# A graph network's first layer, written as a straight pass over chunks with more buffers between the engines

## The chip, the cores and the metric

The kernel runs on one core of a Trainium2 chip. A core has five engines with instruction queues of their own: PE (TensorE, the matrix unit), DVE (VectorE), ACT (ScalarE), POOL (GpSimd) and SP (SyncE). Each works its queue in order, and they meet only through semaphores. DMAs are issued from the queues of SP, ACT and POOL; a gather by a list of row numbers is issued on POOL. SBUF is the on-chip memory of 128 partitions, PSUM the memory that PE writes. The metric is the time of one execution on the device in microseconds (us).

## The reference

The program is four layers of message passing over a graph with 12,500 nodes and 400,000 edges, sorted by target `dst`; a node has 32 features. Ahead of each layer the features are normalized and passed through a relu. Only the first layer matters here:

```python
h = jnp.maximum(_layernorm(x, axis=-1), 0.0)
x = x + _L0_gnn_ref(h, edge_attr_32, L0_gnn_eps, src, dst)

def _L0_gnn_ref(node_feat, edge_feat, eps, src, dst):
    m = jax.nn.relu(node_feat[src] + edge_feat)
    neigh = jax.ops.segment_sum(m, dst, num_segments=node_feat.shape[0])
    return (1.0 + eps[0]) * node_feat + neigh
```

For each edge: fetch the source's row, add the edge's 32 numbers, relu, and add the result to the target's row. The third layer needs the number of edges of each source node (`deg`), which depends on `src` alone, so the kernel counts it in the first layer's pass.

## The kernel before

Edges lie 128 to a tile, one to a partition. There are 3125 tiles of real edges; 16 tiles (`CT`) make a chunk, four tiles (`G`) a group, four groups (`CG`) a chunk, and 196 chunks the pass. Since edges are sorted by target, and a chunk holds 2048 edges, the targets of a chunk lie within 128 consecutive rows, its window; the place of an edge in the window is prepared in `local`, with the window's first row as an integer in the last column (`wbase`). A flag read at the start chooses this fast way (`self.fast`) or a general one, which does not run with these inputs.

For each group the fast pass does this:

- Four indirect DMAs on POOL (L544 in `gather`) fetch 128 rows of 32 numbers each into the tile `hs`.
- `places0`: ACT makes the one-hot tile `oh` (128 edges x 128 places for each of four tiles): four squares of iota minus place (L472) and a relu of 1 - 2x over all of it (L473). What is 0 in the square becomes 1, all else 0.
- `main`: DVE adds `hs` and the edge's numbers into `m` (L678), ACT applies the relu (L679).
- `collect`: four matmuls of `m` with `oh` (L457), in float32, add up in the PSUM tile `ps_win` over the chunk; each shows as two records. The result stands transposed, 32 x 128.
- In `tail` (L684 on), the counting: DVE makes two one-hots in bfloat16, `ohi` and `olo` (L696), of the source's number split into quotient and remainder by 100 (`hi` and `lo`, made by `split_sources`, L480 to L483, once a chunk), and four matmuls (L699) add up their products in the PSUM tile `ps_deg`.

A chunk closes in its last group: ACT copies the sums to `s4` (L461), PE transposes them with an identity matrix (L462), ACT copies the 128 x 32 result to `wsum` (L464), and `put_late` has ACT read the window's first row into a register (L508) and issue the DMA that writes `wsum` into one of four tables of partial sums, which are added after the pass. DVE adds `ps_deg` to `deg` (L702).

The order is set by `edges`, a loop of a single round whose body is written out for all 784 groups. In step g it issues the gathers of group g+4 (`AHEAD`), the one-hots `oh` of group g+1, the message of group g, and the collecting and counting of group g-1. Loads by SP (`src`, `edge_attr_32` and `local`) run up to two chunks (`LEAD`) further ahead. In every second step after the first 16 one step of work for later layers (`rest`) is put in: loads, splits of float32 into bfloat16 parts, unit vectors. That order is the program's; a scheduler then places each engine's instructions by dependences and free buffers, and adds the semaphores.

The buffers between the engines are rotating: a tile's name has so many places, and a new tile waits until the instructions that read the one in its place are done. They are: `hs` six groups; `oh` and `m` three groups; `ohi` and `olo` two groups; `hi`, `lo` and `s4` two; `wsum` four; `ps_win` and `ps_deg` two chunks each; the loads six chunks.

Of the kernel before, what the change touches and what calls it, by code (L numbers as in the profile page):

```python
# [8 lines left out]
F32 = mybir.dt.float32  # L9
BF16 = mybir.dt.bfloat16  # L10
# [46 lines left out]
class GNN:  # L57
# [393 lines left out]
    def collect(self, l, pool, psum, c, feat, t0):  # L451

        nc = self.nc
        if t0 == 0:
            c["sum"] = psum.tile([P, P + D], F32, name="ps_win")
        for k in range(G):
            nc.tensor.matmul(c["sum"][:D, :P], lhsT=feat[:, k, :], rhs=c["oh"][:, k, :],  # L457
                             start=t0 + k == 0, stop=t0 + k == self.CT - 1)
        if t0 + G == self.CT:
            s4 = pool.tile([D, P], F32, name="s4")  # L460
            nc.scalar.copy(s4, c["sum"][:D, :P])  # L461
            nc.tensor.matmul(c["sum"][:, P:], lhsT=s4, rhs=self.eye[:D, :D], start=True, stop=True)  # L462
            s = pool.tile([P, D], F32, name="wsum", bufs=4)
            nc.scalar.copy(s, c["sum"][:, P:])  # L464
            self.put_late(l, c, s)

    def places0(self, pool, c, t0):

        nc = self.nc
        c["oh"] = pool.tile([P, G, P], F32, name="oh", bufs=3)  # L470
        for k in range(G):
            nc.scalar.activation(c["oh"][:, k, :], self.iota, AF.Square, bias=c["local"][:, t0 + k : t0 + k + 1], scale=-1.0)  # L472
        nc.scalar.activation(c["oh"], c["oh"], AF.Relu, bias=self.one, scale=-2.0)  # L473

    def split_sources(self, pool, c):

        nc, J, CT = self.nc, self.J, self.CT
        hi = c["hi"] = pool.tile([P, CT], F32, name="hi")
        lo = c["lo"] = pool.tile([P, CT], F32, name="lo")
        nc.vector.tensor_scalar(hi, c["src"], -0.5 * (J - 1), 1.0 / J, op0=ALU.add, op1=ALU.mult)  # L480
        nc.vector.tensor_scalar_add(hi, hi, ROUND)
        nc.vector.tensor_scalar_add(hi, hi, -ROUND)
        nc.vector.scalar_tensor_tensor(lo, hi, -float(J), c["src"], op0=ALU.mult, op1=ALU.add)  # L483

# [150 lines left out]
    def layer0(self):  # L635
        nc, tc, J = self.nc, self.tc, self.J
        if not self.fast:
            with tc.tile_pool(name="rest", bufs=1) as pool:
                for _ in self.rest(pool):
                    pass  # L640
        with ExitStack() as ctx:
            rest = None
            if self.fast:
                rest = self.rest(ctx.enter_context(tc.tile_pool(name="rest", bufs=1)))
                for _ in range(TABS[0]):
                    next(rest)
            big = ctx.enter_context(tc.tile_pool(name="big0", bufs=LEAD + 4 if self.fast else 2))
# [4 lines left out]
            flat = ctx.enter_context(tc.tile_pool(name="flat0", bufs=1, space=PSUM))  # L652
            iota = flat.tile([P, P], F32, name="iota_p")
            nc.vector.tensor_copy(iota, self.iota)

            def load(col):
                if self.fast:
                    c = {n: self.load(big, n, col) for n in ("src", "edge_attr_32")}
                else:
                    c = {n: self.load(big, n, col) for n in ("src", "dst", "edge_attr_32")}  # L660
                    c["row"] = self.load_row(big, "dst_t", col)
                    c["rows"] = big.tile([P, self.CT], I32, name="rows")
                c["col"] = col
                return c
# [890 lines left out]
```

## Time and profile before

| what | us |
|---|---|
| median of 3 runs | 20930.95 (20918.97 to 20951.87) |
| the profiled execution | 20928.96 |
| its span | 20927.2 |
| first gather of the first layer | 92.8 |
| last gather of the first layer | 4733.3 |
| last copy to `wsum` of the first layer | 4758.6 |
| first gather of the next stage | 4877 |
| POOL's gathers of the first layer, busy | 3029.8 |
| mean clock granted to TensorE over the span | 0.739 of full |

The span runs from the first to the last instruction on the core. The first layer takes the first 4.7 ms of 20.9; layers two and three together reach to about 15,300 us, and the last layer fills the rest. A row of the groups of instructions has the line in the kernel, the engine, the operation with output and inputs, the count, the busy time and the mean duration of one in ns, and then the idle time of the engine just before them, with what ended it. "Issue" is idle time in which the engine waited for nothing that the profile shows; "remote" is a release that the profile could not put down to an instruction. PEld is the loading of weights into PE, which overlaps its matmuls. POOL's row for a gather is the time to issue it, and its data arrive later.

### The profile page before, as it was taken

The page shows a single profiled execution, that of the slowest core. Times are in us where ns is not written, and L with a number is a line of the kernel's source. Part 1 is how long each engine was busy: PE and PEld are TensorE (multiplying, and loading weights), DVE is VectorE, ACT ScalarE, POOL GpSimd, SP SyncE. Part 2 cuts the span into 40 slices and gives each one's busy share as a digit, 9 for nine tenths or more (in the row PEclk, how much of TensorE's full clock was granted, in tenths as well). Part 3 has the DMA queues.
Part 4 walks back from the last instruction along what each step waited for, and adds up shares of the span by engine and source line. Part 5 has one row for each costly group of instructions (what it writes and reads, how often), then busy time and mean ns, then how long its engine had stood idle before and what let it go on. Part 6 is the DMA issues. An engine that isn't in the chain of part 4 may idle for free.

```text
span 20927.2 us, 193298 instructions
## 1 busy us (share of the span) xinstructions
PE 12665.5 (61%) x56836; PEld 6400.1 (31%) x56836; DVE 12158.2 (58%) x22370; ACT 7811.2 (37%) x17960; POOL 14371.0 (69%) x12508
## 2 busy tenths in 40 slices
PE   3344444434766666666666666666637777777776
PEld 2233333221211111111111111111135555555554
DVE  3333333224766666666666666666746666666666
ACT  2334444332333333333333333333224444444443
POOL 4666666664788888888888888888755555555553
PEclk6555555556777777777777777777768888888887
DMA  2113332112444444444444444444411111111111
GB/s 93 40 43 110 111 97 80 24 23 74 98 90 90 90 90 90 90 90 91 88 90 90 91 90 90 87 90 91 93 35 23 23 22 23 23 23 23 23 23 30
DMA packets 1538780, 1407.21 MB, mean 67 GB/s; under 512 B 1112166, under 2 KB 1307312, under 8 KB 1482824
## 3 DMA queue, kind: packets, MB, share of 16 engines
q1 hardware_dynamic: 724998, 1146.69, 17.4%
q0 software_dynamic: 750000, 205.60, 12.0%
q10 hardware_dynamic: 62704, 42.42, 0.7%
q8 instruction: 448, 7.34, 0.1%
q14 instruction: 630, 5.16, 0.1%
HBM read 1156.82 MB, written 236.20 MB: 67 GB/s over the span
## 4 chain that ended last, share of the span: by engine, by line
DVE 24%; PE 15%; issue 13%; another core or an unknown queue 13%; POOL 11%; ACT 7%; DMA 2%; DVEq 0%; ACTq 0%; SPq 0%; POOLq 0%
DVE z L862 6%; POOL acc L1017 5%; POOL hs L818 5%; PE ps_w L1316 5%; PE ps_y L859 4%; DVE pv L1324 1%; ACT oh L1346 1%; DVE f L1333 1%; DVE pa L1320 1%; PE ps_o L869 1%; ACT X L843 1%; ACT hid L1293 1%; DVE cnt L999 1%; PE ps_sum L1352 1%
## 5 line engine op out<-in xcount | busy, mean ns | idle before, releaser
L1017 POOL DMA_INDIRECT acc<-summed,rows x3125 | 5133.6, 1643 | 995.0 <-issue 886.7
L1280 POOL DMA_INDIRECT hs<-feat,src x3125 | 3008.8, 963 | 2498.0 <-DVE ps L1322 1494.4
L544 POOL DMA_INDIRECT hs<-feat,src x3125 | 3029.8, 970 | 1702.6 <-issue 863.1
L818 POOL DMA_INDIRECT hs<-feat,src x3125 | 3197.8, 1023 | 1195.8 <-issue 945.8
L1316 PE MATMUL ps_w<-w2b,hid 128*128 128x256 f32 x12544 | 3199.8, 412 | 70.5 <-issue 56.8
L862 DVE TENSOR_TENSOR z<-ps_y,hid 128x1024 f32<-128x1024 f32 x2352 | 2837.6, 1214 | 435.3 <-PE ps_y L859 164.6
L859 PE MATMUL ps_y<-X,w2t 64*128 64x512 f32 x4704 | 2377.1, 743 | 1129.8 <-DVE z L862 648.8
L1316 PEld LDWEIGHTS ps_w<-w2b,hid 128*128 128x128 f32 x12544 | 2578.0, 209 | 638.6 <-issue 89.8
L859 PE MATMUL ps_y<-Q,w2t 64*128 64x512 f32 x4704 | 1683.7, 840 | 1642.9 <-DVE z L862 1153.7
L491 ACT CAST f<-f 128x512 bf16<-128x512 f32 x784 | 479.9, 612 | 4773.9 <-DVE f L887 3739.1
L457 PE MATMUL ps_win<-oh,m 128*32 128x128 f32 x6272 | 1430.3, 406 | 819.5 <-ACT m L679 426.6
L869 PE MATMUL ps_o<-z,sums 128*32 128x512 f32 x9408 | 1748.1, 702 | 27.7 <-DVE r L874 16.1
L472 ACT ACTIVATE oh<-iota,local 128x128 f32<-128x128 f32 x3136 | 1018.6, 389 | 1923.2 <-remote 1520.1
L1293 ACT ACTIVATE hid<-ps_h 128x1024 f32<-128x1024 f32 x784 | 800.5, 1021 | 2390.6 <-remote 1992.0
L699 PE MATMUL ps_deg<-olo,ohi 128*125 128x100 bf16 x3136 | 432.6, 287 | 1793.5 <-DVE olo L696 1469.7
L1320 DVE TENSOR_TENSOR pa<-ps_w,q 128x512 f32<-128x512 f32 x784 | 539.9, 689 | 1650.4 <-remote 1476.6
L859 PEld LDWEIGHTS ps_y<-Q,w2t 64*128 64x128 f32 x4704 | 521.9, 256 | 2897.5 <-DVE z L862 1562.2
L833 DVE STREAM_TRANSPOSE X<-hs 128x512 f32<-128x512 f32 x392 | 273.4, 700 | 1943.4 <-DMA hs<-feat,src 1171.6
L859 PEld LDWEIGHTS ps_y<-X,w2t 64*128 64x128 f32 x4704 | 613.2, 210 | 2329.1 <-DVE z L862 1134.0
L457 PEld LDWEIGHTS ps_win<-oh,m 128*32 128x32 f32 x6272 | 946.1, 163 | 1157.6 <-ACT m L679 487.5
L678 DVE TENSOR_TENSOR m<-hs,edge_attr 128x128 f32<-128x128 f32 x784 | 226.9, 289 | 1642.8 <-remote 808.1
L1346 ACT ACTIVATE oh<-iota,local 128x128 bf16<-128x128 f32 x3136 | 1057.3, 391 | 50.7 <-DMA edge_attr<-in_edge_attr 26.3
(212 smaller groups left out, 19053.9 us busy)
## 6 DMA issues: line engine op xcount, KB each, us to landing
has<-loc_t SPq DMA_DIRECT2D x392, 1024.0 KB
srow<-in_src_t SPq DMA_DIRECT2D x392, 512.0 KB
hs<-feat,src POOLq DMA_INDIRECT x9375
N<-n_t SPq DMA_DIRECT2D x3136, 32.0 KB
emb<-pp SPq DMA_DIRECT2D x252, 280.0 KB
emb<-emb SPq DMA_DIRECT2D x196, 360.0 KB
emb<-pp SPq DMA_DIRECT2D x252, 224.0 KB
emb<-emb SPq DMA_DIRECT2D x196, 288.0 KB
```

What stands on the lines that cost most here:

```text
L457: nc.tensor.matmul(c["sum"][:D, :P], lhsT=feat[:, k, :], rhs=c["oh"][:, k, :], start=t0 + k == 0, stop=t0 + k == self.CT - 1)
L472: nc.scalar.activation(c["oh"][:, k, :], self.iota, AF.Square, bias=c["local"][:, t0 + k : t0 + k + 1], scale=-1.0)
L544: self.nc.gpsimd.indirect_dma_start(out=t[:, k, :], out_offset=None, in_=self.feats[l][:], in_offset=bass.IndirectOffsetOnAxis(ap=idx[:, t ...
L818: nc.gpsimd.indirect_dma_start(out=c["hs"][:, k, :], out_offset=None, in_=self.feats[1][:], in_offset=bass.IndirectOffsetOnAxis(ap=c["src" ...
L859: nc.tensor.matmul(y[:, q, :], lhsT=self.w2t[64 * q : 64 * q + 64, h, j, :], rhs=c["Q" if j < 3 else "X"][64 * q : 64 * q + 64, h, :], sta ...
L862: nc.vector.tensor_mul(z, y, c["hid"][:, 2 * h : 2 * h + 2, :])
L869: nc.tensor.matmul(c["o", j // 3][32 * q : 32 * q + 32, :], lhsT=self.sums[:, j, :], rhs=c["z", j, q % 2][:, q // 2, :], start=j % 3 == 0, ...
L1017: nc.gpsimd.indirect_dma_start(out=self.tabs[2][k % NTAB][:], out_offset=bass.IndirectOffsetOnAxis(ap=c["rows"][:, G * g + k : G * g + k + ...
L1280: nc.gpsimd.indirect_dma_start(out=c["hs"][:, k, :], out_offset=None, in_=self.feats[3][:], in_offset=bass.IndirectOffsetOnAxis(ap=c["src" ...
L1293: nc.scalar.activation(c["hid"][:, m, :, 2 * h : 2 * h + 2, :].rearrange("p b q s -> p q b s"), t.rearrange("p q (b s) -> p q b s", s=32), ...
L1316: nc.tensor.matmul(w[:, k, :], lhsT=c["hid"][:, m, 4 * g + k].rearrange("p q s -> p (q s)"), rhs=self.w2b[:, m, :], start=m == 0, stop=m == 1)
L1346: nc.scalar.activation(c["oh"][:, k, :], self.iota, AF.Square, bias=c["local"][:, k : k + 1], scale=-1.0)
```

## The change

The first layer's fast pass no longer goes through `edges`. A new function, `edges0`, writes it out by chunks, with pools of its own; the general way stays in `any0`. Each chunk has one `hs` tile of 16 x 32 numbers a partition, in four places, and its gathers are issued two chunks ahead, one group beside each group computed; loads go three chunks ahead. The tiles `oh`, `m`, `ohi` and `olo` have ten places each, `hi`, `lo` and `s4` three, `ps_win` and `ps_deg` three each. In a group the order is: gathers, one-hots `oh`, message, counting, collecting, all of the same group. The deg add, the copy to `s4` and the transpose of a chunk are issued after the third group of the next chunk, the copy to `wsum` and the write after its fourth. The instructions themselves and their shapes stay as they were.

```diff
-    def collect(self, l, pool, psum, c, feat, t0):
...
-    def places0(self, pool, c, t0):
...
-    def split_sources(self, pool, c):
...
     def layer0(self):
+        nc = self.nc
+        if self.fast:
+            self.edges0()
+        else:
+            self.any0()
+        with self.tc.tile_pool(name="end0", bufs=1) as pool:
+            agg = self.gather_sum(0, pool)
+            nc.vector.tensor_add(self.x, self.x, agg)
+            nc.vector.scalar_tensor_tensor(self.x, self.h, self.eps1, self.x, op0=ALU.mult, op1=ALU.add)
++    def edges0(self):
+
+        nc, tc, J, CT, NW = self.nc, self.tc, self.J, self.CT, self.NW
+        with ExitStack() as ctx:
+            rest = self.rest(ctx.enter_context(tc.tile_pool(name="rest", bufs=1)))
+            for _ in range(TABS[0]):
+                next(rest)
+            ld = ctx.enter_context(tc.tile_pool(name="load0", bufs=6))
+            gp = ctx.enter_context(tc.tile_pool(name="gather0", bufs=4))
+            mp = ctx.enter_context(tc.tile_pool(name="group0", bufs=10))
+            wp = ctx.enter_context(tc.tile_pool(name="work0", bufs=3))
+            psum = ctx.enter_context(tc.tile_pool(name="psum0", bufs=3, space=PSUM))
+            hist = ctx.enter_context(tc.tile_pool(name="hist0", bufs=3, space=PSUM))
+            flat = ctx.enter_context(tc.tile_pool(name="flat0", bufs=1, space=PSUM))
+            iota = flat.tile([P, P], F32, name="iota_p")
+            nc.vector.tensor_copy(iota, self.iota)
+
+            def fetch(c):
+                c["src"] = self.load(ld, "src", c["col"])
+                c["ea"] = self.load(ld, "edge_attr_32", c["col"])
+                c.update(self.places_of(ld, c["no"]))
+
+            def gather(c, g):
+                if g == 0:
+                    c["hs"] = gp.tile([P, CT, D], F32, name="hs")
+                    self.rows_for(c["hs"], CT, c, 0)
+                for k in range(G * g, min(G * g + G, self.filled(c))):
+                    nc.gpsimd.indirect_dma_start(
+                        out=c["hs"][:, k, :], out_offset=None, in_=self.feats[0][:],
+                        in_offset=bass.IndirectOffsetOnAxis(ap=c["src"][:, k : k + 1], axis=0))
+
+            def split(c):
+                hi = c["hi"] = wp.tile([P, CT], F32, name="hi")
+                lo = c["lo"] = wp.tile([P, CT], F32, name="lo")
+                nc.vector.tensor_scalar(hi, c["src"], -0.5 * (J - 1), 1.0 / J, op0=ALU.add, op1=ALU.mult)
+                nc.vector.tensor_scalar_add(hi, hi, ROUND)
+                nc.vector.tensor_scalar_add(hi, hi, -ROUND)
+                nc.vector.scalar_tensor_tensor(lo, hi, -float(J), c["src"], op0=ALU.mult, op1=ALU.add)
+
+            def places(c, g):
+                c["oh", g] = mp.tile([P, G, P], F32, name="oh")
+                for k in range(G):
+                    nc.scalar.activation(c["oh", g][:, k, :], self.iota, AF.Square,
+                                         bias=c["local"][:, G * g + k : G * g + k + 1], scale=-1.0)
+                nc.scalar.activation(c["oh", g], c["oh", g], AF.Relu, bias=self.one, scale=-2.0)
+
+            def message(c, g):
+                gs = slice(G * g, G * g + G)
+                m = c["m", g] = mp.tile([P, G, D], F32, name="m")
+                nc.vector.tensor_add(m, c["hs"][:, gs, :], c["ea"][:, gs, :])
+                nc.scalar.activation(m, m, AF.Relu)
+
+            def count(c, g):
+                if g == 0:
+                    c["deg"] = hist.tile([P, P], F32, name="ps_deg")
+                ohi = mp.tile([P, G, NP], BF16, name="ohi")
+                olo = mp.tile([P, G, J], BF16, name="olo")
+                for oh, v, n in ((ohi, c["hi"], NP), (olo, c["lo"], J)):
+                    nc.vector.tensor_tensor(oh, iota[:, None, :n].to_broadcast([P, G, n]),
+                                            v[:, G * g : G * g + G, None].to_broadcast([P, G, n]), op=ALU.is_equal)
+                for k in range(G):
+                    nc.tensor.matmul(c["deg"][:NP, :J], lhsT=ohi[:, k, :], rhs=olo[:, k, :],
+                                     start=G * g + k == 0, stop=G * g + k == CT - 1)
+
+            def collect(c, g):
+                if g == 0:
+                    c["sum"] = psum.tile([P, P + D], F32, name="ps_win")
+                for k in range(G):
+                    nc.tensor.matmul(c["sum"][:D, :P], lhsT=c["m", g][:, k, :], rhs=c["oh", g][:, k, :],
+                                     start=G * g + k == 0, stop=G * g + k == CT - 1)
+
+            def turn(c):
+                nc.vector.tensor_add(self.deg, self.deg, c["deg"][:NP, :J])
+                s4 = wp.tile([D, P], F32, name="s4")
+                nc.scalar.copy(s4, c["sum"][:D, :P])
+                nc.tensor.matmul(c["sum"][:, P:], lhsT=s4, rhs=self.eye[:D, :D], start=True, stop=True)
+
+            def write(c):
+                s = wp.tile([P, D], F32, name="wsum", bufs=4)
+                nc.scalar.copy(s, c["sum"][:, P:])
+                self.put_late(0, c, s)
+
+            cs = [{"no": c, "col": c * CT} for c in range(NW)]
+            for c in range(3):
+                fetch(cs[c])
+            for c in range(2):
+                for g in range(CG):
+                    gather(cs[c], g)
+            for c in range(NW + 1):
+                if c + 3 < NW:
+                    fetch(cs[c + 3])
+                for g in range(CG):
+                    if c + 2 < NW:
+                        gather(cs[c + 2], g)
+                    if c < NW:
+                        if g == 0:
+                            split(cs[c])
+                        places(cs[c], g)
+                        message(cs[c], g)
+                        count(cs[c], g)
+                        collect(cs[c], g)
+                    if c and g == 2:
+                        turn(cs[c - 1])
+                    if c and g == 3:
+                        write(cs[c - 1])
+                    if c > 3 and g % 2:
+                        next(rest, None)
+            for _ in rest:
+                pass
+
+    def any0(self):
...
-            big = ctx.enter_context(tc.tile_pool(name="big0", bufs=LEAD + 4 if self.fast else 2))
+            big = ctx.enter_context(tc.tile_pool(name="big0", bufs=2))
...
-            self.edges(load, gather, front, main, tail,
-                       windowed=(lambda c, row: c.update(self.places_of(big, row))) if self.fast else None, beside=rest)
...
+            self.edges(load, gather, front, main, tail)
```

The loads, `places_of` and `put_late` are as before. Lines of `any0` that are left out serve the general way alone.

## The prediction

> **What bounds the kernel now.** I read the groups of instructions first, for the work of the changed stage. The columns behind the bar are busy time, mean ns of one, and the engine's idle time before them with what ended it.
>
> ```profile
> L544 POOL DMA_INDIRECT hs<-feat,src x3125 | 3029.8, 970 | 1702.6 <-issue 863.1
> L457 PE MATMUL ps_win<-oh,m 128*32 128x128 f32 x6272 | 1430.3, 406 | 819.5 <-ACT m L679 426.6
> L472 ACT ACTIVATE oh<-iota,local 128x128 f32<-128x128 f32 x3136 | 1018.6, 389 | 1923.2 <-remote 1520.1
> ```
>
> Gathers on POOL cost 3029.8 us, plus 863.1 us between issues that wait for nothing: 3892.9 us is the floor of this stage on POOL, 1.246 us a gather, 19.9 us a chunk of 16. The first gather starts at 92.8 us and the last partial sum is copied at 4758.6 us: 4666 us, 23.8 us a chunk. No other engine is near that. Of 1000 us without side work:
>
> ```profile
> 3600.00:4600.00 1000.00, 408.97 (x2128) 298.55 (x2126) 262.81 (x717) 369.05 (x1105) 645.78 (x685) 0.57 0.13 25
> ```
>
> Busy us are PE, weight loads, DVE, ACT, POOL; then PE's granted clock and the DMA share. At 23.4 us a chunk this is 9.6 us of PE, 6.1 of DVE, 8.6 of ACT, each under half of POOL's 19.9. So POOL should never wait; the waits from 200 to 4700 us (total, times, longest) show that it does, and who waits longer:
>
> ```profile
> ACT oh L472 <- remote: 1469.2, 162, 14.9
> DVE deg L702 <- remote: 884.1, 86, 15.2
> POOL hs L544 <- issue: 837.2, 2655, 2.1
> DVE m L678 <- remote: 787.8, 146, 13.7
> POOL hs L544 <- DVE m L678: 345.3, 114, 17.4
> POOL hs L544 <- DVE hi L480: 224.3, 62, 6.9
> ```
>
> The last two rows and smaller ones of the kind are POOL waiting for a place in hs that DVE's add m frees; the idle time there less "issue" is 727 us. One chunk in order of time (start, duration, idle before and its releaser):
>
> ```profile
> 4303.82 0.66 PE L699 MATMUL ps_deg<-olo,ohi 128*125 128x100 bf16 x8
> 4307.24 3.89 PE L457 MATMUL ps_win<-oh,m 128*32 128x128 f32 x16 [2.75 <-ACT oh L472]
> 4316.38 0.94 POOL L544 DMA_INDIRECT hs<-feat,src  x1 [0.30 <-issue]
> 4318.94 0.26 DVE L702 TENSOR_TENSOR deg<-deg,ps_deg 125x100 f32<-125x100 f32 x1 [14.52 <-remote]
> 4320.41 1.28 ACT L472 ACTIVATE oh<-iota,local 128x128 f32<-128x128 f32 x4 [10.63 <-remote]
> 4320.47 0.29 DVE L678 TENSOR_TENSOR m<-hs,edge_attr 128x128 f32<-128x128 f32 x1 [1.27 <-remote]
> 4321.03 0.94 POOL L544 DMA_INDIRECT hs<-feat,src  x1 [3.71 <-DVE hi L480]
> ```
>
> PE's counting matmuls are recorded as over at 4304.5 and its collecting ones at 4311.1, but the deg add that reads the first starts at 4318.94, and the squares that need one of three oh buffers at 4320.41. In between every compute engine idles while POOL gathers. Then 4.65 us pass between two gathers instead of 1.25, since the next m is late. This returns once a chunk. "Remote" names no releaser; those instructions need only PE's results, so I read it as PE's completions being seen 10 to 14 us late during a run of gathers.
>
> The last layer lets me test that. There the chunk's sums are copied at these times:
>
> ```profile
> 20729.58 0.26 ACT L1355 COPY s<-ps_sum 96x128 f32<-96x128 f32 x1 [4.63 <-PE ps_sum L1352]
> 20757.33 0.26 ACT L1355 COPY s<-ps_sum 96x128 f32<-96x128 f32 x1 [2.95 <-PE ps_sum L1352]
> 20762.36 0.94 POOL L1280 DMA_INDIRECT hs<-feat,src  x1 [0.30 <-issue]
> 20776.37 0.26 ACT L1355 COPY s<-ps_sum 96x128 f32<-96x128 f32 x1 [2.82 <-PE ps_sum L1352]
> 20794.64 0.26 ACT L1355 COPY s<-ps_sum 96x128 f32<-96x128 f32 x1 [2.82 <-PE ps_sum L1352]
> 20812.45 0.26 ACT L1355 COPY s<-ps_sum 96x128 f32<-96x128 f32 x1 [2.82 <-PE ps_sum L1352]
> ```
>
> With gathers a chunk takes 27.8 us; after the last gather 18.3 and 17.8. So a chunk's 20 us of gathers cost that layer some 10 us of a compute that has few buffers.
>
> [...]
>
> **The change, part by part.** The work per chunk is the same instructions: 16 gathers, 16 squares, 4 and 4 relus, 4 adds, 8 one-hots, 16+16 matmuls, one transpose, two copies, one deg add, three loads, one register read and write-out. What changes is when each may start.
>
> (1) Ten buffers instead of three for oh and m, and of two for ohi and olo. A group's buffers come free when PE's completion is seen, 10 to 14 us after the work. Three groups are what ACT makes in 3 x 2.3 = 7 us (4 squares 1.27, relus 0.7 and 0.3), so it runs dry for the 10.63 us shown. Ten groups are 23 us of ACT at full rate, or 2.5 chunks, 50 us, at POOL's pace; that covers 14 us either way. The waits of squares and m for "remote" then go. What is late next is (2).
>
> (2) The closing. Before, ACT's copy s4, DVE's deg add and the transpose stand directly behind the chunk's last matmul, in order, so everything queued behind them waits as long as PE's completion is late: 884 us at deg, 253 at s4, 560 at the copy to wsum in the 4500 us. Now they stand three groups into the next chunk, 15 us later at POOL's pace (7 us if compute catches up). Behind s4 then wait the last group's squares on ACT, behind deg the next m on DVE, behind the transpose the last group's counts on PE. 15 us covers most of a lateness of 10 to 14; if it does not, ACT still has 19.9 - 8.6 = 11 us a chunk to spare. Three buffers each of ps_win and ps_deg let PE begin the next two chunks before the wsum copy. On path: 0; without that cover, up to the 14.5 us of the deg row in a chunk, which is rival B or D.
>
> (3) Gathers two chunks ahead into four places of a whole chunk, against 4 groups ahead into six. No gather is added or dropped, and nothing else is queued on POOL, so its floor stays 3892.9 us. A place now comes free after a chunk's fourth add instead of each group's, but with 48 tiles in hand and not 20. On path: 0 to a wait of POOL like the last layer's (rival D).
>
> (4) SP's loads: the same three a chunk, three chunks ahead, six buffers as before. SP waits 630 us for local's place (freed by ACT's register read), always ahead of need, since POOL's waits name no load but 44.6 us of landing gathers. Price 0; without the cover at most those 44.6 us again.
>
> (5) Counting before collecting: 0.6 us of counts (4 x 0.15) move ahead of 1.9 us of collecting in PE's order; hidden, as PE has 10 us a chunk idle. The loop of one round with its run-time addresses becomes straight code: the trace has no row for it alone. Bounds: the 92.8 us ahead of the first gather on one side, and the same again lost in fetching code on the other; I take 0, because the same instructions are unrolled in both, and because the instruction queues move 12.5 MB over the whole run at 0.1% each.
>
> (6) Side work for later layers keeps two steps a chunk; the stage's period is the same with it and without it (408.97 against 405 and 417 us of PE per 1000 us at 500 and 2000 us).
>
> The clock of PE: 0.57 of full, with idle stretches of 11 us a chunk. [...]
>
> Sum. POOL's waits of 727 us, and about 20 outside 200 to 4700, could all go: 747 us. How many do? The last layer gives a rate for compute during gathers: 20 us of gathers delay it by 10, so it goes at half speed. ACT's 8.6 to 9.6 us a chunk at half speed need 17 to 19 of POOL's 19.9: just enough, with little to spare. So I keep some pauses, 0.5 us a chunk or 100 us, and take 747 - 100 = 645. Profiled execution 20928.96 us (span 20927.2 and 1.8 around it), 2 us under the median of the runs: 20930.95 - 645 = 20,285 us.
>
> **The rivals.**
>
> A, the forecast: POOL-bound, 20.0 to 20.8 us a chunk: 20,180 to 20,340. For it: spare time on every engine, and buffers for 50 us against 14.
>
> B, PE's completions need pauses of POOL to be seen at all. For it: in the shown chunk they come 1.6 to 3 us after the run's last gather (4317.3). Against it: within runs some come after 2 to 9 us. Then pauses remain, but one may serve two chunks, as there are two chunks of gathers ahead: half of 727 is won, 20,565; bounds 20,340 and 20,880.
>
> C, no change: the pause needed goes with the number of gathers, not with the buffers. For it: the period is the same with and without side work. Then 3.7 us stay in each chunk: 20,890 to 20,970.
>
> D, slower: with four whole-chunk places POOL runs longer without a pause, and ACT, held in order at s4, can't run on, so that the longer runs are paid back in longer pauses. The last layer, with the same gathers two chunks ahead and four places, shows it:
>
> ```profile
> L1280 POOL DMA_INDIRECT hs<-feat,src x3125 | 3008.8, 963 | 2498.0 <-DVE ps L1322 1494.4
> ```
>
> That is 7.6 us a chunk. It decides when the pause passes 3.8 us a 16 gathers; between that and 7.6 the stage loses up to 196 x 3.8 = 745 us, the middle 370: 21,300, nearest bound 20,980. Against it: that layer has 18 us of compute a chunk and this one 9.6, and ten buffers to run on.
>
> **How the numbers follow.** A 0.46, B 0.28, C 0.09, D 0.17. A measurement of this kernel can tell about 0.2%, 42 us, from no change. Faster: A and B, 0.74 and a little of C, 0.75; within: most of C, 0.07; slower: D and the end of C, 0.18. The range from 20,170 (the floor 20,184, less a little for part 5) to 20,975 leaves out most of D and some 0.02 below; with cases of both signs, A's own range is 20,180 to 20,340.
>
> **What would show it.** Right, if from 500 to 4500 us gathers follow each other 1.25 us apart with POOL's busy share near 75% (0.944 of 1.25), the wait for DVE m is under 100 us, the squares' "remote" is under 300, and the last gather ends near 4090 us. For (2): the deg add's idle time is near nothing or ends at places without a POOL gap. B shows as gaps of 3 us every 32 gathers; C as the same 3.7 us every 16; D as runs of more than 16 with gaps over 4 us, and s4 or deg at the head of the waits. The other layers must stay within 20 us. The forecast is wrong if lateness grows with the length of a run, for then no number of buffers is enough.

## The result and the profile after

The changed kernel is slower: 21,245.65 us (median, 21,219.94 to 21,263.61) against 20,932.08 us of the kernel before, a ratio of 1.0148 with a 95% interval of 1.013 to 1.0166. A second comparison, in a later series of runs, gave 1.0153 (1.0136 to 1.0169). The profiled execution took 21,234.09 us, its span 21,232.3.

All of it lies in the first layer. Its last gather starts at 5025.1 us where it was 4733.3, which is 292 us later, and the next stage's first gather at 5177.6 where it was 4877.2, 300 us later; the whole span grew by 305. A chunk takes 25.3 us and not 23.7.

In the groups of instructions of the changed kernel the rows that answer to those of before are these (busy, mean ns of one, idle just before with what ended it):

```profile
L639 POOL DMA_INDIRECT hs<-feat,src x3125 | 2998.7, 960 | 2025.5 <-issue 909.5
L661 DVE TENSOR_TENSOR m<-hs,edge_attr 128x128 f32<-128x128 f32 x784 | 227.8, 291 | 3115.1 <-issue 2076.0
L654 ACT ACTIVATE oh<-iota,local 128x128 f32<-128x128 f32 x3136 | 994.4, 387 | 254.7 <-issue 172.8
```

The squares have what the prediction promised them: their idle time fell from 1923.2 to 254.7 us, since a buffer for oh is nearly always free. But POOL's idle time, less the part that waits for nothing, grew from 839.5 to 1116.0 us. That is 276 us, and nearly all of the loss. The waits from 200 to 4700 us say where it went (total, times, longest):

```profile
DVE m L661 <- issue: 1937.6, 268, 30.3
ACT wsum L691 <- remote: 1724.7, 87, 36.8
POOL hs L639 <- DVE m L661: 836.1, 96, 24.3
DVE m L661 <- remote: 553.0, 65, 23.6
```

The first row names nobody, but 205 of its 268 waits, 1758 us of it, end within 0.15 us after PE raised its semaphore: these too are waits for PE's results. Of the same kind of row in the kernel before, it was 511 of 577 us.

The wait for PE has not gone; it has moved. ACT now waits at the copy to wsum, up to 36.8 us at a time, where before it waited at the squares, at most 14.9. One stretch in order of time shows what that does to POOL:

```profile
4017.45 0.40 PE L687 MATMUL ps_win<-eye,s 32*128 32x32 f32 x2
...
4032.50 0.26 DVE L684 TENSOR_TENSOR deg<-deg,ps_deg 125x100 f32<-125x100 f32 x1 [8.13 <-remote]
...
4043.35 0.94 POOL L639 DMA_INDIRECT hs<-feat,src  x1 [0.30 <-issue]
4046.64 0.29 DVE L661 TENSOR_TENSOR m<-hs,edge_attr 128x128 f32<-128x128 f32 x1 [13.89 <-remote]
...
4048.71 0.18 ACT L691 COPY wsum<-ps_win 128x32 f32<-128x32 f32 x1 [36.30 <-remote]
4048.86 0.29 DVE L661 TENSOR_TENSOR m<-hs,edge_attr 128x128 f32<-128x128 f32 x1 [0.62 <-remote]
...
4054.05 0.29 DVE L661 TENSOR_TENSOR m<-hs,edge_attr 128x128 f32<-128x128 f32 x1 [2.75 <-ACT oh L656]
...
4057.27 0.29 DVE L661 TENSOR_TENSOR m<-hs,edge_attr 128x128 f32<-128x128 f32 x1 [1.38 <-ACT oh L654]
...
4057.83 0.94 POOL L639 DMA_INDIRECT hs<-feat,src  x1 [13.53 <-DVE m L661]
```

PE's transpose is recorded as over at 4017.85, yet ACT sees it at 4048.71, 31 us later. Until 4044.29 of that time POOL gathers: it issues 32 tiles from 4003.44 on with one break of 1.5 us, the last at 4043.35. Only 2.3 us after that run ends does the first m come, and ACT is free 2.1 us later still. Then four groups of computing are needed before POOL may go on, because a place in hs is now a whole chunk and comes free with its fourth m: 4046.64, 4048.86, 4054.05, 4057.27. With places of a group the first m would have been enough.

Counted over the layer, with gaps under 2 us not taken for pauses:

| | runs of 16 gathers | pause after, mean us | runs of 32 | pause after, mean us |
|---|---|---|---|---|
| before | 111 | 3.81 | 0 | |
| after | 102 | 4.90 | 42 | 12.24 |

A run of 32 takes 39.7 us, and 51.9 with its pause, which is 26.0 us a chunk.

### The profile page after: what moved, and what is told of

Read it like the earlier page. It is cut to its first block, busy times and chain, and to the rows that moved or that the text cites. A ratio compares the mean times of both kernels' runs of the same rounds, so it can differ in the third digit from the quotient of the medians.

```text
span 21232.3 us, 192790 instructions
## 1 busy us (share of the span) xinstructions
PE 12578.8 (59%) x56836; PEld 6320.3 (30%) x56836; DVE 12164.9 (57%) x22368; ACT 7758.4 (37%) x17960; POOL 14346.0 (68%) x12508
## 4 chain that ended last, share of the span: by engine, by line
DVE 22%; PE 15%; issue 12%; another core or an unknown queue 11%; POOL 10%; ACT 9%; DMA 2%; ACTq 0%; DVEq 0%; SPq 0%; POOLq 0%
DVE z L930 6%; POOL acc L1085 5%; PE ps_w L1384 5%; POOL hs L886 5%; PE ps_y L927 4%; DVE pv L1392 1%; PE ps_o L937 1%; ACT oh L1414 1%; ACT oh L654 1%; ACT X L911 1%; DVE pa L1388 1%; DVE f L1401 1%; PE ps_sum L1420 1%; DVE cnt L1067 1%
## 5 line engine op out<-in xcount | busy, mean ns | idle before, releaser
L680 PE MATMUL ps_win<-oh,m 128*32 128x128 f32 x6272 | 1295.4, 372 | 455.7 <-issue 219.2
L673 PEld LDWEIGHTS <-ohi 128*125 128x125 bf16 x3136 | 384.1, 196 | 2913.3 <-issue 1494.7
L654 ACT ACTIVATE oh<-iota,local 128x128 f32<-128x128 f32 x3136 | 994.4, 387 | 254.7 <-issue 172.8
```

The lines of the kernel that those rows point to most:

```text
L654: nc.scalar.activation(c["oh", g][:, k, :], self.iota, AF.Square, bias=c["local"][:, G * g + k : G * g + k + 1], scale=-1.0)
L673: nc.tensor.matmul(c["deg"][:NP, :J], lhsT=ohi[:, k, :], rhs=olo[:, k, :], start=G * g + k == 0, stop=G * g + k == CT - 1)
L680: nc.tensor.matmul(c["sum"][:D, :P], lhsT=c["m", g][:, k, :], rhs=c["oh", g][:, k, :], start=G * g + k == 0, stop=G * g + k == CT - 1)
```

## The experiments

Each series of runs used one chip, and the kernel before ran beside the others each time. Its median was 20,774 us in the first series, 18,834 in the second, 20,778 in the third, 20,959 in the fourth and 20,926 in the fifth. All ratios below are within a series, and times that were expected in us are meant against the 20,932 of the first comparison. The second one differs in kind, and that is a result of its own.

**Without gathers, and with gathers that nobody reads.** Both make m from the edge's numbers alone; the first issues no gather in the first layer.

```diff
-                nc.vector.tensor_add(m, c["hs"][:, gs, :], c["ea"][:, gs, :])
+                nc.vector.tensor_add(m, c["ea"][:, gs, :], c["ea"][:, gs, :])
```

> The changed kernel without the first layer's gathers: m is made from the edge's numbers alone (added to themselves), so the layer's sums are not the reference's; all else is as in the changed kernel. It measures what a chunk of computing costs when no gather runs. If runs of gathers are what delays PE's completions: no wait named remote of more than 1 us, and 10 to 13 us a chunk (ACT's 8.6 to 9.9 us of work and a little), the layer about 2.3 ms instead of 4.95, the whole about 18,500 us. If the lateness has another cause (instruction fetch, the order of the work): waits of 10 us and more stay, and the chunk takes 18 us or more, the whole 19,800 or more.

> The changed kernel with all its gathers, but nothing reads what they fetch (m is the edge's numbers added to themselves, so the sums are not the reference's). POOL is never held, so it gathers without a pause for some 3.9 ms, and the computing beside it is held by nothing but itself. If PE's completions are held for as long as gathers follow each other: while they go on a chunk of computing takes 28 to 60 us, ACT's copy to wsum and DVE's m wait for PE, and the chunks left at 4.0 ms run at 10 to 13 us each; the whole 20,300 to 21,300 us. If unbroken gathers delay a completion by a bounded 10 to 14 us, as the prediction took it: computing keeps ahead of the gathers, under 20 us a chunk, the layer ends with the gathers near 4.0 ms, the whole about 20,250 us or less.

Without gathers a chunk took 9.73 us in the median (10.57 in the mean), the whole 18,223.67 us, and no wait named remote was left. None of PE's 941 results from 200 to 2100 us reached its semaphore more than 0.015 us after the recorded end of the matmul. With free gathers a chunk took 26.8 us in the mean, the whole 21,560.76 us, a little above the range of the first theory. POOL was not quite free, since it still waited for its lists of sources (741.0 us from 200 to 3700). But it mostly ran 32, 48 or 64 gathers at a time, and the longest waits for PE from 200 to 3700 us grew with that:

```profile
DVE m L661 <- remote: 1822.4, 105, 69.4
ACT wsum L691 <- remote: 943.9, 37, 70.8
```

So the lateness is not bounded by 10 to 14 us: the longest wait named remote was 15.3 us in the kernel before, with most runs at 16 gathers, 36.8 in the changed kernel, with runs of 32 among them, and 70.8 here, with runs of mostly 32 to 64. By an estimate from the 20 us that 16 gathers take, the 10 to 14 us of the kernel before fit the rest of such a run.

**The closing at once.**

```diff
-                    if c and g == 2:
-                        turn(cs[c - 1])
-                    if c and g == 3:
-                        write(cs[c - 1])
+                    if c < NW and g == 3:
+                        turn(cs[c])
+                        write(cs[c])
```

> The changed kernel with one part undone: a chunk is closed at the end of its own fourth group, as before, and not in the next chunk. If the late closing (ACT and DVE held in order at a completion of the chunk before) is what costs the 310 us: back to 20,950 or below. If the longer runs of gathers (two chunks ahead, places of a whole chunk) cost it: 21,150 to 21,400, as the change stays.

21,039.57 us, ratio 1.0127 (1.011 to 1.0144), which is 21,198 us against 20,932 and so in the second range. The interval overlaps that of the changed kernel: the medians are 0.2% apart, the far ends of the intervals 0.6%. By the medians the late closing is a small part of the loss. POOL still had runs of 32 and pauses of 10.6 us after them. ACT's long wait stood at the copy to s4 instead, from 200 to 3700 us:

```profile
ACT s L686 <- remote: 1286.2, 54, 36.6
```

**The buffers alone, in the kernel before.**

```diff
-        c["oh"] = pool.tile([P, G, P], F32, name="oh", bufs=3)
+        c["oh"] = pool.tile([P, G, P], F32, name="oh", bufs=10)
```

and the same for m, ohi and olo.

> The kernel before with the buffers alone: ten places for oh, m, ohi and olo, all else as it was (its gathers by groups, four groups ahead, its closing at once). If three buffers were what made POOL wait, as the prediction took it: 20,300 to 20,600. If the pauses are needed for PE's completions to be seen, or the closing holds ACT and DVE in the same place: 20,880 to 20,970, no change. If more buffers alone lengthen the runs and the waits: above 21,050.

20,793.78 us, ratio 1.001 (1.000 to 1.0019): no gain, as in the second case expected. Where the squares had waited 1469.2 us, the waits from 200 to 4700 us are now at the next instructions that need PE:

```profile
DVE m L678 <- issue: 1380.0, 285, 17.3
ACT s L461 <- remote: 1000.8, 127, 19.8
ACT wsum L464 <- remote: 900.6, 88, 18.0
```

The buffers, on which the whole gain of the prediction stood, buy nothing here: ACT must still read each chunk's sum, and it is there that it waits now.

**Places of a group, one chunk ahead.** The changed kernel with hs by groups in six places, as before, and the rest of the change kept.

```diff
-            gp = ctx.enter_context(tc.tile_pool(name="gather0", bufs=4))
+            gp = ctx.enter_context(tc.tile_pool(name="gather0", bufs=AHEAD + 2))
...
+                c["hs", g] = self.gather(gp, "hs", 0, c["src"], G * g, c)
```

> The changed kernel with its gathers as before: hs by groups in six places, one chunk ahead, instead of whole chunks in four places, two chunks ahead; ten buffers and the late closing stay. If the longer runs of gathers and the later freeing of a whole chunk's place cost the 1.5%: ratio to before 0.995 to 1.005, runs of 16 to 24 gathers, pauses of 3 to 4 us. If the order inside the group or the late closing costs it: 1.010 to 1.015 stays.

> The changed kernel with its gathers by groups in six places, one chunk ahead, again. Where PE's completions are prompt: 0.998 as measured. Where they are late: if whole-chunk places (freed by a chunk's fourth add, 10 us of computing after a pause instead of 2.5) and runs of 32 gathers cost the 1.5%, the ratio is 0.995 to 1.005; if the order in the group or the late closing costs it, 1.010 to 1.015.

In the second series, where nothing was late, 18,803.47 us and a ratio of 0.9982 (0.9973 to 0.9992). In the third 20,764.68 us, 0.9995 (0.9986 to 1.0005), beside the changed kernel itself:

> The changed kernel once more, beside the kernel before. In the last four runs PE's completions were not late at all during gathers (one run of 3002 gathers with 9.8 us a chunk of computing beside it), and the kernel before took 18,834 us there, against 20,932 and 20,774 in the runs ahead of them. So the lateness is not always there. If it is absent again (the kernel before near 18,830 us): both versions wait for POOL alone, 19.9 to 20.4 us a chunk, and the ratio is 0.996 to 1.003. If it is there (the kernel before near 20,800): 1.011 to 1.018 as at first. If the change costs 1.5% by its order whatever PE does: 1.015 in both cases.

21,094.21 us, 1.0153 (1.0136 to 1.0169). So the whole loss is in the arrangement of the gathers. Which part of it, the next run tells.

**As many tiles ahead, but places of a group.** Sixteen places of a group hold as many tiles as four of a chunk, and the gathers are two chunks ahead as in the change.

```diff
-            gp = ctx.enter_context(tc.tile_pool(name="gather0", bufs=4))
+            gp = ctx.enter_context(tc.tile_pool(name="gather0", bufs=16))
...
+                c["hs", g] = self.gather(gp, "hs", 0, c["src"], G * g, c)
```

> The changed kernel with one thing different: hs in sixteen places of a group instead of four of a chunk, so that as many tiles are gathered as far ahead, and only the freeing is finer. If it is the late freeing that costs 1.5% (46 pauses of 10 to 15 us, in which four groups must be computed before one place comes free): ratio to before 0.995 to 1.004, no pauses over 10 us. If the longer runs cost it (32 gathers without a pause): 1.010 or more, and the long pauses stay.

20,923.02 us, ratio 0.998 (0.9968 to 0.9992). POOL's waits from 200 to 4700 us in this kernel:

```profile
POOL hs L510 <- DVE m L655: 482.8, 124, 17.4
POOL hs L510 <- DVE hi L640: 59.3, 17, 4.4
```

against 836.1 in the changed kernel; with all smaller rows of the kind it is 740 us against 1001, and 727 in the kernel before. Nearly all runs had 12 to 28 gathers, with pauses of 3 to 5 us in the mean. It is the late freeing of a whole chunk's place that costs the 1.5%. Tiles ahead cost nothing: with them the rest of the change, taken together, wins 0.2%.

**Two chunks closed together.** An attempt to need no completion of PE for eight groups: hs in ten places of a group, the closing of two chunks at the start of the next two, one count tile for both.

```diff
+                if c and c % 2 == 0:
+                    turn(cs[c - 2])
+                    turn(cs[c - 1])
+                    write(cs[c - 2])
+                    write(cs[c - 1])
```

> A version built on the reading that PE's completions are seen only in a pause of POOL or soon after: gathers by groups in ten places, the closing of two chunks together at the start of the next two (one count tile for both), so that ACT and DVE need no completion of PE for eight groups. If one pause of 3.5 us then serves 32 gathers: 39.9 + 3.5 = 43.4 us for two chunks, 21.7 us a chunk, 196 x 1.7 = 330 us below before, ratio 0.982 to 0.986. If PE itself is slowed while gathers run, its backlog of two chunks is not done by the pause and the gain goes: ratio 0.995 to 1.01.

> The version that closes two chunks together, again. Where PE's completions are prompt: 0.997 as measured. Where they are late: if one pause serves 32 gathers, 21.7 us a chunk, ratio 0.982 to 0.988; if PE's backlog of two chunks is not done by the pause, 0.995 to 1.01.

18,781.73 us (0.9973, 0.9963 to 0.9983) in the second series, 20,760.79 us (0.9995, 0.9985 to 1.0004) in the third. There most runs had 12 to 24 gathers, with pauses of 3 to 4.5 us, and ACT still waited for PE at the copy to s4, up to 34.2 us. In this version one pause does not serve two chunks.

**An unbroken run.** All gathers use one fixed list and nobody reads them, so POOL waits for nothing.

```diff
-                        in_offset=bass.IndirectOffsetOnAxis(ap=c["src"][:, k : k + 1], axis=0))
+                        in_offset=bass.IndirectOffsetOnAxis(ap=src0[:, k : k + 1], axis=0))
```

> As the kernel with free gathers (computing does not read what they fetch), and now every gather uses one fixed list of sources, so that POOL waits for no load either: an unbroken run of 3125 gathers, some 3.9 ms. It measures the rate of computing while gathers never pause (without gathers: 9.7 us a chunk). If a run of gathers holds PE's completions only until it pauses: computing all but stands still until 3.9 ms, more than 60 us a chunk, and the rest of the 196 chunks then takes 9.7 us each; the layer 5.3 to 5.8 ms, the whole 21,400 to 22,000 us. If it slows PE to a rate instead: a steady period, from the 48-gather runs (3 chunks in 75 us, 29 us of work less 23 done in the pause and the first 10 us, over some 50 us) 0.1 to 0.3 of full speed, 32 to 90 us a chunk, without one long stop. The two are told apart by the longest wait for PE: some ms against under 100 us.

> The unbroken run of 3125 gathers with computing beside it, again. Where PE's completions are prompt: 9.8 us a chunk beside the gathers, as measured, the layer 4.4 ms. Where they are late: 32 to 90 us a chunk if PE is slowed to a rate, all but a standstill until 3.9 ms if its completions wait for a pause; the layer 4.9 to 5.8 ms.

In the second series, 19,108.56 us: one run of 3002 gathers without a break, and computing beside it nearly as if they were not there, 149 chunks by 1799 us, 11.2 us each. (It then stood still until 4000 us: DVE's filling of the last chunk's empty tiles, which comes in order there, waited 2215 us for its place in hs.) In the third series, with the same program, 22,240.99 us: 23 chunks by 4416 us, 180 us each. Busy time from 500 to 1500 us (PE, weight loads, DVE, ACT, POOL, then PE's granted clock, the DMA share, GB/s), first in the second series:

```profile
500.00:1500.00 1000.00, 772.99 (x5271) 599.33 (x5268) 907.30 (x2254) 868.49 (x2547) 771.41 (x751) 0.79 0.58 175
```

and in the third:

```profile
500.00:1500.00 1000.00, 66.14 (x356) 53.38 (x354) 76.50 (x219) 43.12 (x130) 771.57 (x716) 0.50 0.12 28
```

POOL was as busy in both, and PE did a twelfth of the work. The waits of the third series from 500 to 3900 us name PE's results:

```profile
ACT wsum L692 <- remote: 2004.3, 13, 211.3
DVE m L662 <- remote: 1485.4, 38, 61.1
```

Neither theory of the expectation is quite right. It is no full stop: the trace has 66 updates of PE's semaphore between 500 and 4000 us, 45 us apart in the median. As a rate it is a sixteenth of full speed (180 us a chunk against 11.2 in the second series), below the 0.1 to 0.3 expected. Results come in step with the gathers: of 127 waits of ACT and DVE over 5 us from 500 to 3900 us, 101 end within 0.2 us after a gather's end (by chance it would be some 18, an estimate from one gather every 1.39 us), and 92 of these after the same one of every four gathers. In the changed kernel, with its shorter runs, no such step is seen.

**The collecting in bfloat16.** The same with oh and m in bfloat16, where a collecting matmul shows as one record and not two. (In the kernel before, its 3136 matmuls in float32 show as 6272 records, the 3136 of the counting in bfloat16 as 3136.)

> [...] If PE has worked in time and only its completions are seen late: the period stays within 10% of the run before.

> [...] Where completions are late: if PE itself is slowed while gathers run, the chunk's period falls from 190 us by a third or more, and over 35 chunks are done at 4.4 ms; if only completions are held, 21 to 26 chunks as before (23). Where they are prompt: 9.7 us a chunk as measured, and nothing told apart.

19,064.6 us in the second series, where a chunk took 9.65 us in the median against 9.84. In the fourth, 22,201.99 us and 34 chunks by 4421 us, 123 us each, against 23 and 180. That falls between the two theories. With half the collecting's records a chunk took less, so PE's own progress seems to be slowed and not only the news of it, but 34 is just short of what was set for that, an estimate of the author's, and the two runs are from different series. PE's records don't decide it: in the unbroken run of the third series the eight records of one group start 0.21 us apart, the last is over at 648.67, and the semaphore is raised at 689.39; but the ends of matmuls are modelled. It stays open.

**Short and long pauses.** Free gathers, with a filler on POOL (an iota that nothing uses): 1.00 us after every 4 gathers, or 3.57 us after every 16 (shown); hs and the loads have fewer places to make room.

```diff
+                if g == CG - 1:
+                    w = waits.tile([P, 4096], BF16, name="wait")
+                    nc.gpsimd.iota(w, pattern=[[1, 4096]], base=0, channel_multiplier=0,
+                                   allow_small_or_imprecise_dtypes=True)
```

> The free gathers by one fixed list, with a filler on POOL of about 1 us after every 4 gathers (nothing else uses it; hs and the loads have fewer places to make room). If completions get through in any idle time of the gathers, in proportion: as much computing as with the long pauses, some 4 us in 24. If a pause must be long enough for the gathers under way to land (completions came 3.0 us after a run's last gather): next to none, 100 us a chunk or more until the gathers end near 4.7 ms, the whole above 22,000 us. Where PE's completions are prompt: 10 to 12 us a chunk, the whole near 19,100 us, and nothing told apart.

> The same with one filler of about 4 us after every 16 gathers, so the same idle time in one piece. If a pause of 3 us and more lets all pending completions through: one chunk or so of computing for each pause as in the kernel before, 23 to 30 us a chunk, so that most of the 196 chunks are done when the gathers end near 4.7 ms, the whole 20,900 to 21,300 us. If it is not the pause but the end of all gathers that counts, or the filler keeps POOL as busy as a gather does: 100 us a chunk or more, the whole above 22,000.

Fourth series, where completions were late: 20,825.09 and 20,765.06 us. The gathers of a chunk took 23.8 us on average in both, but beside them a chunk of computing took 14.2 us with the short pauses and 20.7 us with the long ones, where 23 to 30 were expected (180 without any, in the third series). Busy time from 500 to 2500 us with the short pauses:

```profile
500.00:2500.00 2000.00, 1297.23 (x7492) 987.78 (x7493) 1205.09 (x2919) 1323.01 (x3890) 1641.77 (x1653) 0.66 0.41 121
```

and with the long ones:

```profile
500.00:2500.00 2000.00, 901.43 (x5004) 692.16 (x5003) 878.27 (x2124) 829.43 (x2436) 1604.37 (x1418) 0.58 0.28 78
```

So here a pause of 1 us after every 5 us of gathers let most of the computing through (14.2 us a chunk, against 9.7 without gathers), and many short ones did more than one long one (14.2 against 20.7). That answers the expectation of the first run against its second theory. It also shows that it is not POOL's busy time that holds PE: with the short fillers POOL was busy for 82% of the time and a chunk took 14.2 us, in the unbroken run of the third series for 77%, and a chunk took 180.

**Pauses put in on purpose.** The kernel with sixteen places of a group, with fillers in the first and in the last layer, kept in their order on POOL.

```diff
+    def pause(self, pool, n):
+        w = pool.tile([P, n], BF16, name="wait")
+        self.tc.keep_in_program_order(self.nc.gpsimd.iota(
+            w, pattern=[[1, n]], base=0, channel_multiplier=0, allow_small_or_imprecise_dtypes=True))
```

> The version with sixteen places of a group, and on POOL a filler of about 0.6 us (an iota of 512 that nothing uses, kept in order) after every 4 gathers, in the first and in the last layer. If short pauses let PE's completions through: first layer 4 x (4 x 1.25 + 0.45) = 21.8 us a chunk instead of 23.4, 300 us less; last layer 22 to 24 instead of 27, 600 to 1000 us less; ratio 0.935 to 0.965. If a pause must be as long as a gather to count: no gain, the fillers are lost (350 us a layer), ratio 1.00 to 1.03. Where completions are prompt (the kernel before near 18,830 us): the fillers only cost, ratio 1.02 to 1.04.

> The same with a filler of 0.6 us after every 8 gathers in the first layer (20.9 us a chunk if it is enough, 23 or more if it is not) and of 1.0 us after every 4 in the last layer (23.6 us a chunk if it is enough, 27 if it is not). Ratio 0.935 to 0.965 if both are, 1.0 or more if neither is; which layer gained is read from the stages. Where completions are prompt: 1.02 to 1.04.

20,293.37 us, ratio 0.9694 (0.9678 to 0.9711), and 20,176.67 us, ratio 0.9644 (0.9628 to 0.966). Both beat the kernel before; the first just misses its range, the second lies inside it. The gain is not in the first layer, where 21.8 and 20.9 us a chunk were forecast: it took 22.98 and 23.16 us there in the mean, against 23.16 in the same kernel without fillers. Why 0.6 us after 4 or 8 gathers does so little there is not shown. It is in the last layer, where a chunk fell from 27.47 us to 24.34 with 0.6 us and to 23.79 with 1.0 us after every 4 gathers. (The fillers came with gathers kept in order on POOL; that order was not run without them.) There POOL's waits from 15,700 us to 20,700 were, in the kernel before,

```profile
POOL hs L1280 <- DVE ps L1322: 1397.3, 180, 11.9
POOL hs L1280 <- issue: 822.3, 2698, 0.3
```

and, from 15,700 to 20,000, in the version with 1.0 us after every 4 gathers

```profile
POOL hs L1356 <- issue: 772.9, 2867, 0.3
POOL hs L1356 <- DVE f L459: 2.1, 13, 0.2
```

POOL waits for nobody any more: gathers and fillers set that layer's time. Between the first and the last copy to wsum of that layer lie 4640 us now and 5356 in the profile of the kernel before; these 716 us are nearly all of the 750 won.

## Why the prediction was wrong

**The bound and the waits** were read rightly: the layer ends with POOL, POOL waits for places in hs, and these wait for PE's results seen late. The cause given for the lateness, a run of gathers, was shown by taking the gathers away: 9.7 us a chunk and no result over 0.015 us late.

**Where the time went.** The result is some 960 us above the forecast of 20,285. Of these, 645 are the gain set down for part (1), which did not come. The other 315 are lost by part (3), which the forecast had put at nothing: some 350 us, less the 0.2% that the rest of the change wins.

**Part (1)** failed at its size. It took the lateness as 10 to 14 us, whatever the run, and set buffers for 50 us against it. The waits of the squares did go, and the deg add's idle time fell from 1046.7 to 109.0 us (200 to 4700), as part (2) had it. These two signs of being right came true while the time went the other way, because the wait had moved. The lateness grows with the run: the longest wait is 36.8 us in the changed kernel, 70.8 with free gathers, 211.3 in the unbroken run. The buffers alone changed nothing (1.001).

**Part (2)** named the price without its cover, up to 14.5 us in a chunk, and what is queued behind s4; the cover of 15 us failed with the bound on the lateness. The place was off by one instruction, wsum and not s4. Undoing it wins some 0.2% of the 1.5, so the order of the closing is not where most of the loss lies.

**Part (3)** is the step that lost the time. It saw that a place comes free only after a chunk's fourth add, and set this at nothing because more tiles are in hand. The tiles in hand are used up in any pause; what counts then is how much computing stands between PE's result and POOL's next gather. That is one add with places of a group and four groups with a place of a chunk: 10.9 us from the first m at 4046.64 to the fourth's end at 4057.56. The run with sixteen places of a group shows it alone: 0.998 instead of 1.015, some 350 us.

**Parts (4) to (6)** held. POOL's waits name no load but 6.1 us of landing gathers from 200 to 4700 (DVE's for `src` rose from 121.1 to 168.9 us), the later stages kept their time within 16 us, and the clock granted to PE was 0.55 to 0.62 in the stretches looked at, where it was 0.55 to 0.57 before.

**The sum** rested on computing at half speed during gathers, drawn from the last layer. In an unbroken run it was a sixteenth (180 us against 11.2). The half was an average over 20 us of gathers and 8 us of pause, and it could not be carried to longer runs.

**The rivals.** D came true, with 0.17. Its time of 21,300 us was only 54 us too high, but that was the middle of a span of some 700 us, so the closeness is luck. Its condition, a pause over 3.8 us for 16 gathers, was met (4.9 after 16, 12.2 after 32). Its mechanism was half right: places of a chunk, yes, but the greater number of tiles ahead costs nothing. C's mechanism, a pause that goes with the number of gathers and not with the buffers, is what the buffers alone show (1.001). B was tested by closing two chunks together: there one pause did not serve two. What the prediction said would make it wrong, a lateness that grows with the run, is what the runs showed.

## What to carry to other kernels

Before buffers are bought against a late result, find out what ends the lateness. Here the results came late beside gathers and not without them; ten buffers in the place of two and three changed nothing (1.001), and the wait moved from the squares (1469.2 us) to the copies to s4 and wsum (1000.8 and 900.6). Free a place as finely as it is filled: here 10.9 us lay between the first m after a pause and the first freed place of a whole chunk, and with places of a group the ratio was 0.998 instead of 1.015. And where one engine's stream goes with late results on another, try a short pause put in on purpose: 1.0 us after every 4 gathers took 3.7 us off each chunk of the last layer (27.47 to 23.79). It was worth it only where the results were late: in the second series that layer took 20.7 us a chunk without any filler, less than the 23.8 with them.

## What was not expected of the hardware

Beside back-to-back gathers issued by POOL, 1.25 to 1.39 us apart, the results of matmuls came late: the longest waits named remote were 15.3 us in the kernel before, 36.8 in the changed kernel and 211.3 in the unbroken run of the third series, and without gathers no result came more than 0.015 us late. Those of DVE and ACT were not late in the stretches looked at: in the changed kernel POOL goes on at 4057.83 us, 0.27 us after the m that it waits for ends, and in the kernel before PE starts at 3222.48 us, beside gathers, 0.05 us after the relu of m on ACT ends. A chunk of computing took 9.7 us without gathers and 180 us beside an unbroken run. With a filler of 1.00 us on POOL after every 4 gathers it took 14.2 us.

In one series of five none of this happened: the same program ran 11.2 us a chunk beside 3002 unbroken gathers, and the kernel before took 18,834 us there, against 20,774 to 20,959 in the others. A chunk of the last layer took 20.7 us in the kernel with places of a group, against 26.9 in the third series. The length of a gather does not explain it: 0.97 us in both series in the kernel with places of a group, 0.97 and 1.07 in the unbroken run. Nor does the fetching of instructions: a 16-KB packet of it took 1.08 us in the unbroken run of the second series and 0.97 in that of the third (500 to 1500 us). Nor is it the chip alone, if its number tells chips apart: the record names number 12 for the first series and for the second, half an hour later. What makes the difference is open. The changed kernel did not run in that series, nor was it tried whether it gains there; that POOL was hardly held in the versions which did run there (20.3 and 20.4 us a chunk, against 19.9 of gathers alone) suggests that all of them would end close together. Whether PE itself is slowed or its results are only passed on late is open too, and so is whether the issuing of gathers does it or the moving of their rows.
